# Gated attention followed by graph attention on one core: all five engines in a hand-written order, five x buffers

## The chip, the cores and the metric

The kernel runs on one core of one Trainium2 chip. The metric is the device time of that core in microseconds (us) for one launch over the whole batch.

## The reference

The inputs are `x` (64 graphs of 256 nodes with 512 channels, f32) and an adjacency matrix `adj` (64 x 256 x 256, int32). Cut to what matters:

```python
h = relu(layernorm(x))                                  # layer 0
q, k, v = h @ Wq.T, h @ Wk.T, h @ Wv.T                   # 8 heads of 64 channels
c = softmax(where(adj, q @ k.T / 8, -inf)) @ v
gate = sigmoid(concat(c, h) @ Wg.T + bg)
x = x + gate * h + (1 - gate) * c
h = relu(layernorm(x))                                  # layer 1
Wh = h @ W
e = leaky_relu((Wh @ a1)[:, None] + (Wh @ a2)[None, :])
x = x + elu(softmax(where(adj, e, -1e9)) @ Wh)
```

## The kernel before, in words

All work is in f32. A graph's 256 nodes fill two tiles of 128 partitions. The five dense products (q with k, v, gate, Wh) are done by a Strassen-like scheme, `strassen`: seven products (`product`, line 149) instead of eight, in three PSUM banks `ma`, `mb`, `mc`. Each of these banks has one buffer. The scheme is cut into three parts: products 1, 6, 5, then 7, 2, then 4, 3. VectorE (`add`, line 159) and ScalarE (lines 163 and 173) read partial results out of the banks, and the next product into the same bank, or into that bank for the next dense product, has to wait for them. The other PSUM tiles share a pool `w` with five buffers. The sums of operand blocks are made by GpSimd for activations (`token_sums`, lines 133 to 136) and by VectorE for weights (`weight_sums`, lines 104 to 107, once at the start).

The batch is a software pipeline. Round `i` works on four graphs: `p = i + 1` (transposes of h, q, k, v), `i` (attention), `q = i - 1` (gate, residual, second norm, Wh) and `r = i - 2` (graph attention, output). In round `i` the kernel loads graph `i + 2` into an x buffer, and `p_norm` makes its mask, its statistics and h. The graph is stored from the same buffer at the end of `g_out` four rounds later, when it is graph `r`. The x pool has four buffers and the adj pool one. So the load of graph `i + 2` writes the buffer from which graph `i - 2` is stored in the same round.

The order of TensorE's instructions is the written order of `emit_round`. The order on VectorE (DVE), ScalarE (ACT), GpSimd (POOL) and SyncE (SP) is set by a planner with costs and priorities:

```python
    with tc.manual_schedule(engines={mybir.EngineType.PE}):
```

Names that the prediction uses, with the lines of the kernel before: `norm_stats` (188 to 195), h (203), copies out of PSUM (122 on ScalarE, 124 on VectorE), scores `ps` (276), softmax over scores (294 the masked minimum on VectorE, 298 the exponential on ScalarE, 302 the reciprocal on VectorE, 306 the scaling on GpSimd), transposed probabilities `ptr` and `ptr_l` (315), weighted sum `pc` (336), the difference `d` of `g_mix` (365), the edge terms of `g_edges` (396 to 409), the output products `po` (420) and the ELU with the store (425 to 432).

At the start all twelve weight transfers, the two rows of `a` and the bias are issued on ScalarE's queue (lines 97, 115, 118), and all weight sums and edge columns (line 486) are traced ahead of the first round.

Of the kernel before, what the change touches and what calls it, by code (L numbers as in the profile page):

```python
# [8 lines left out]
F32 = mybir.dt.float32  # L9
I32 = mybir.dt.int32  # L10
BF16 = mybir.dt.bfloat16
AF = mybir.ActivationFunctionType
ALU = mybir.AluOpType
# [9 lines left out]
def kernel(  # L23
# [41 lines left out]
    def pool(name, bufs, **kw):  # L65
# [2 lines left out]
    const = pool("const", 1)  # L68
    st = pool("st", 4)
    sb = {tag: pool(tag, bufs) for tag, bufs in {  # L70
        "x": 4, "adj": 1, "mask": 4, "hT": 3, "S": 3, "qk": 3, "v": 2, "wh": 1, "e": 4, "eT": 4,
        "cT": 1, "z": 1, "tmp": 9, "U": 3,
    }.items()}
    ps = {tag: pool(f"ps_{tag}", bufs, space=bass.MemoryType.PSUM) for tag, bufs in {
        "ma": 1, "mb": 1, "mc": 1, "w": 5,
# [13 lines left out]
        nc.sync.dma_start(at, adj[g].rearrange("(t p) n -> p t n", p=P))  # L89
        graphs[g] = {"x": xt, "adj": at}  # L90

    load_graph(0)

    def load_weight(name, src, extra):
        w = const.tile([P, HC, 2, HH + extra], F32, name=name)
        for n in range(2):
            nc.scalar.dma_start(w[:, :, n, :HH], src[:, n * HH:(n + 1) * HH].rearrange("(c p) f -> p c f", p=P))
        return w

    def weight_sums(name, w):  # L100

        t = const.tile([P, 3, 2, w.shape[3]], F32, name=f"{name}_t")
        b11, b12, b21, b22 = (w[:, r:r + 2, n, :] for r in (0, 2) for n in range(2))
        nc.vector.tensor_tensor(t[:, 1], b22, b12, ALU.subtract)
        nc.vector.tensor_tensor(b12, b12, b11, ALU.subtract)
        nc.vector.tensor_tensor(t[:, 0], b22, b12, ALU.subtract)
        nc.vector.tensor_tensor(t[:, 2], b21, t[:, 0], ALU.subtract)
        return {1: b11, 2: b21, 3: b22, 4: t[:, 2], 5: b12, 6: t[:, 0], 7: t[:, 1]}

    sources = {"q": wqT, "k": wkT, "v": wvT, "gc": wgT[:H], "gh": wgT[H:], "1": w1}  # L110
    loaded = {key: load_weight(f"w{key}_sb", src, key == "1") for key, src in sources.items()}
    weight = {}
    a_sb = [sb["tmp"].tile([P, H], F32, tag="t", name=f"a_sb_{side}") for side in range(2)]
    for side in range(2):
        nc.scalar.dma_start(a_sb[side], bass.AP(tensor=a.tensor, offset=a.offset + side * H, ap=[[0, P], [1, H]]))
    hbg = const.tile([P, HC], F32, name="hbg")
    with nc.allow_non_contiguous_dma(reason="512 biases, once"):
        nc.scalar.dma_start(hbg, bg.rearrange("(c p) -> p c", p=P))

    def evac(dst, src, on_act):  # L120
        if on_act:
# [61 lines left out]
    def norm_stats(xt, name):  # L183

        mv = st.tile([P, NT, 2], F32, tag="mv", name=f"mv_{name}")
        for t in range(NT):
            bs = st.tile([P, 6], F32, tag="bs", name=f"bs_{name}_{t}")
            nc.vector.bn_stats(bs, xt[:, t, :])  # L188
            nc.vector.bn_aggr(mv[:, t, :], bs)
        ve = st.tile([P, NT], F32, tag="ve", name=f"ve_{name}")  # L190
        nc.vector.tensor_scalar_add(ve, mv[:, :, 1], EPS)  # L191
        rs = st.tile([P, NT], F32, tag="rs", name=f"rs_{name}")
        nc.gpsimd.tensor_tensor(rs, ve, mhalf, ALU.pow)  # L193
        nb = st.tile([P, NT], F32, tag="nb", name=f"nb_{name}")
        nc.vector.scalar_tensor_tensor(nb, mv[:, :, 0], -1.0, rs, ALU.mult, ALU.mult)  # L195
        return rs, nb

    def norm_relu(xt, name):
        rs, nb = norm_stats(xt, name)
        hs = []  # L200
        for t in range(NT):
            h = sb["tmp"].tile([P, H], F32, tag="t", name=f"h_{name}_{t}")
            nc.scalar.activation(h, xt[:, t, :], AF.Relu, bias=nb[:, t:t + 1], scale=rs[:, t:t + 1])  # L203
            hs.append(h)
        return hs
# [11 lines left out]
        return hT  # L217


    def p_norm(g):  # L220
        s = graphs[g]
        mask = sb["mask"].tile([P, NT, N], BF16, tag="t", name=f"mask_{g}")
        nc.vector.tensor_scalar(mask, s["adj"], 0.0, MASKED, ALU.is_equal, ALU.mult)
        s["mask"] = mask
        s["h"] = norm_relu(s["x"], f"l0_{g}")

    def p_transpose(g):
        s = graphs[g]
# [50 lines left out]
                    )  # L279
        s["ps"] = psc  # L280

    def a_softmax(g, half):
        s = graphs[g]
        psc, mask = s.pop("ps"), s["mask"]
        es = s["e", half] = {}
        for jj in range(2):
            low, sums, rec = (
                st.tile([P, 2, NT], F32, tag=tag, name=f"{tag}_{g}_{half}_{jj}") for tag in ("low", "sums", "rec")
            )
            for i in range(2):  # L290
                e = sb["e"].tile([P, NT, N], F32, tag="t", name=f"e_{g}_{half}_{jj}_{i}")
                es[jj, i] = e
                for t in range(NT):
                    nc.vector.tensor_tensor_reduce(  # L294
                        e[:, t, :], psc[jj, i][:, t, :], mask[:, t, :], -SCALE, HUGE, ALU.add, ALU.min,
                        accum_out=low[:, i, t:t + 1],
                    )
                    nc.scalar.activation(  # L298
                        e[:, t, :], e[:, t, :], AF.Exp, bias=low[:, i, t:t + 1], scale=-1.0,
                        accum_out=sums[:, i, t:t + 1],  # L300
                    )
            nc.vector.reciprocal(rec, sums)  # L302
            for i in range(2):
                for t in range(NT):
                    e = es[jj, i]
                    nc.gpsimd.tensor_scalar(  # L306
                        e[:, t, :], e[:, t, :], rec[:, i, t:t + 1], 1.0, ALU.mult, ALU.mult
                    )

    def transpose_probs(e, pool, name, on_act):  # L310

# [37 lines left out]
    def g_gate(g):  # L349
# [5 lines left out]
            f"z_{g}", [P, 2, P], on_channels([(weight["gh"], s["hS"]), (weight["gc"], s["cS"])]), dst  # L355
        )

    def g_mix(g):

        s = graphs[g]  # L360
        hT, cT, z = s["hT"], s["cT"], s["z"]
        for half in (1, 0):
            js = slice(2 * half, 2 * half + 2)
            d = sb["tmp"].tile([P, 2, N], F32, tag="t", name=f"d_{g}_{half}")
            nc.gpsimd.tensor_tensor(d, hT[:, js, :], cT[:, js, :], ALU.subtract)
            for j in (2 * half, 2 * half + 1):
                nc.scalar.activation(z[:, j, :], z[:, j, :], AF.Tanh, bias=hbg[:, j:j + 1], scale=0.5)  # L367
            nc.vector.scalar_tensor_tensor(d, z[:, js, :], 1.0, d, ALU.add, ALU.mult)
            nc.vector.scalar_tensor_tensor(z[:, js, :], d, 0.5, cT[:, js, :], ALU.mult, ALU.add)

    def g_residual(g):
        s = graphs[g]
        for t in range(NT):
            py = ps["w"].tile([P, H], F32, tag="t", name=f"py_{g}_{t}")
            for j in range(HC):
                nc.tensor.transpose(py[:, j * P:(j + 1) * P], s["z"][:, j, t * P:(t + 1) * P], ident)
            nc.vector.tensor_tensor(s["x"][:, t, :], s["x"][:, t, :], py, ALU.add)
        s["h1"] = norm_relu(s["x"], f"l1_{g}")

    def g_transpose_h(g):  # L380
        s = graphs[g]
# [53 lines left out]
    def emit_round(i):  # L435
# [8 lines left out]
        def part(fn, g, n):  # L444
            if 0 <= g < B:
                if n == 0:
                    parts[fn] = fn(g)
                parts[fn][n]()

        p, q, r = i + 1, i - 1, i - 2  # L450
        part(g_gate, q, 0)
        step(g_edges, r)
        part(g_gate, q, 1)
        step(p_transpose, p)
# [1 line left out]
        step(g_mix, q)  # L456
        step(g_transpose, r)
        step(a_transpose, i, 0)
        part(p_qk, p, 0)
        step(g_residual, q)  # L460
        step(g_out, r, 0)
        part(p_qk, p, 1)
        step(a_scores, i, 1)
        step(a_softmax, i, 1)
        step(g_out, r, 1)
        part(p_qk, p, 2)
        step(g_transpose_h, q)
        part(p_v, p, 0)
        step(a_weigh, i, 0)
        part(p_v, p, 1)  # L470
        step(a_transpose, i, 1)
        part(p_v, p, 2)
        step(g_sums, i)
        step(p_norm, p + 1)
        part(g_wh, q, 0)
        step(a_weigh, i, 1)
        part(g_wh, q, 1)
        step(a_scores, p, 0)
        part(g_wh, q, 2)
        step(a_softmax, p, 0)  # L480

    p_norm(0)
    for c in range(HC):
        for side in range(2):
            scr = sb["tmp"].tile([P, 2, HH], F32, tag="t", name=f"scr_{c}_{side}")
            nc.vector.scalar_tensor_tensor(
                scr, loaded["1"][:, c, :, :HH], 1.0, a_sb[side].rearrange("p (n f) -> p n f", n=2),
                ALU.mult, ALU.mult, accum_out=loaded["1"][:, c, side, HH:],
            )
    for key, w in loaded.items():  # L490
        weight[key] = weight_sums(f"w{key}_sb", w)
    nc.vector.tensor_scalar_mul(hbg, hbg, 0.5)

    with tc.manual_schedule(engines={mybir.EngineType.PE}):
        for i in range(-1, B + 2):
            if 0 <= i + 2 < B:
                load_graph(i + 2)
            emit_round(i)
            graphs.pop(i - 2, None)

# [31 lines left out]
```

## Time and profile before

| What | us |
|---|---|
| median of 3 runs | 3758.28 (3757.03 to 3759.89) |
| the profiled execution's own time | 3759.92 |
| its span | 3758.1 |
| TensorE busy (matmul) | 3614.4 |
| VectorE busy | 1968.9 |
| ScalarE busy | 1641.7 |
| GpSimd busy | 1626.0 |

The span runs from the first to the last instruction in the trace; about 1.8 us lie around it. All busy times are of the one core. A matmul's end in the trace is modelled, so two groups of matmuls that overlap in the table of time are running back to back. TensorE does nearly all of its work in f32, and each f32 matmul shows as two instructions; transposes show as one.

### The profile page before, as it was taken

Reading aid. Unit: us, or ns where it says so; the run is one execution under the profiler, and the core shown is the slowest. Engines: PE = TensorE matmul, PEld = TensorE weight load, DVE = VectorE, ACT = ScalarE, POOL = GpSimd, SP = SyncE. Lnnn points to the kernel's source line nnn. Section 1 sums busy time; section 2 is a strip of 40 time slices with the busy share of each in tenths; the row PEclk is TensorE's granted clock in tenths of the full one; section 3 lists DMA queues with packets and bytes.
Section 4 is the critical chain, followed back from the end, with each engine's and each line's share of the span. In section 5 each row is a group of like instructions: output and inputs, shape, how many; then the busy total and the mean of one; then the engine's idle time right before and its main releaser. Section 6 shows DMA issues by size and latency. Waiting matters only on the chain.

```text
span 3758.1 us, 68100 instructions
## 1 busy us (share of the span) xinstructions
PE 3614.4 (96%) x26496; PEld 3118.1 (83%) x26496; DVE 1968.9 (52%) x5609; ACT 1641.7 (44%) x4353; POOL 1626.0 (43%) x2439
## 2 busy tenths in 40 slices
PE   5999999999999999999999999999999999999997
PEld 5888888888888888888888888888888888888885
DVE  4555555555555455555555555555555545555554
ACT  2444444444444444444444444444444444444443
POOL 2444444444444443544444444435444444444443
PEclk9999999999999999999999999999999999999998
DMA  3000000000000000000000000000000000000000
GB/s 110 4 29 26 18 29 26 18 26 24 24 26 18 29 26 18 26 29 18 26 19 29 26 18 29 26 18 26 28 19 26 18 29 26 18 26 29 15 18 17
DMA packets 59697, 95.06 MB, mean 25 GB/s; under 512 B 3824, under 2 KB 26352, under 8 KB 59376
## 3 DMA queue, kind: packets, MB, share of 16 engines
q1 hardware_dynamic: 52224, 83.90, 6.8%
q10 hardware_dynamic: 7152, 6.82, 0.6%
q8 instruction: 209, 3.42, 0.4%
q14 instruction: 112, 0.92, 0.1%
HBM read 57.15 MB, written 33.55 MB: 24 GB/s over the span
## 4 chain that ended last, share of the span: by engine, by line
PE 36%; issue 21%; POOL 15%; DMA 11%; DVE 9%; ACT 8%; POOLq 0%; ACTq 0%; DVEq 0%
PE pmb_z L149 6%; PE pma_z L149 6%; DMA x<-in_x_dram 6%; PE pmb_wh L149 6%; POOL e L306 5%; DMA out_dram<-x 5%; ACT e L298 4%; PE ps L276 3%; PE pc L336 3%; PE pmc_z L149 3%; PE pmc_wh L149 3%; ACT h_l L203 2%; POOL rs_l L193 2%; POOL x L430 2%; DVE bs_l L188 2%
## 5 line engine op out<-in xcount | busy, mean ns | idle before, releaser
L306 POOL TENSOR_SCALAR e<-e,rec 128x256 f32<-128x256 f32 x1024 | 497.2, 504 | 314.9 <-DVE rec L302 299.6
L298 ACT ACTIVATE e<-e,low 128x256 f32<-128x256 f32 x1024 | 505.5, 495 | 115.5 <-DVE low L294 115.5
L193 POOL TENSOR_TENSOR rs_l<-ve_l,mhalf 128x2 f32<-128x2 f32 x128 | 90.4, 706 | 956.3 <-DVE ve_l L191 956.3
L203 ACT ACTIVATE h_l<-x,nb_l,rs_l 128x512 f32<-128x512 f32 x256 | 194.5, 807 | 635.4 <-DVE nb_l L195 630.3
L294 DVE CUSTOM_DVE_ANT_0 e<-ps,mask 128x256 f32<-128x256 f32 x1024 | 369.0, 416 | 69.7 <-PE ps L276 67.0
L430 POOL TENSOR_TENSOR x<-x,pos 128x512 f32<-128x512 f32 x128 | 162.7, 1271 | 246.4 <-DVE pos L429 246.4
L122 ACT COPY eT<-ptr 128x512 f32<-128x512 f32 x512 | 261.5, 593 | 11.1 <-PE ptr L315 3.7
L276 PE MATMUL ps<-qk 64*128 64x256 f32 x2048 | 255.7, 389 | 0.0
L315 PE MATMUL ptr<-ident,e 128*128 128x128 f32 x2048 | 247.9, 274 | 3.9 <-POOL e L306 2.7
L420 PE MATMUL po<-wh,eT_l 128*128 128x512 f32 x512 | 249.1, 609 | 2.0 <-DVE low L294 1.2
L336 PE MATMUL pc<-eT,v 128*64 128x256 f32 x2048 | 249.3, 385 | 0.0
L188 DVE BATCH_NORM_STATS2 bs_l<-x 128x6 f32<-128x512 f32 x256 | 168.5, 679 | 140.0 <-DMA x<-in_x_dram 140.0
L315 PEld LDWEIGHTS ptr<-ident,e 128*128 128x128 f32 x2048 | 230.2, 141 | 13.3 <-POOL e L306 6.4
L122 ACT COPY cT<-pc 128x512 f32<-128x512 f32 x128 | 74.9, 585 | 372.8 <-PE pc L336 372.8
L405 ACT ACTIVATE eg<-eg,nm 128x256 f32<-128x256 f32 x128 | 64.0, 501 | 381.3 <-DVE nm L402 381.3
L276 PEld LDWEIGHTS ps<-qk 64*128 64x128 f32 x2048 | 187.3, 186 | 46.8 <-issue 22.1
L336 PEld LDWEIGHTS pc<-eT,v 128*64 128x64 f32 x2048 | 135.6, 136 | 98.2 <-issue 42.7
L149 PE MATMUL pmb_wh<-w_sb_t,S_l 128*128 128x257 f32 x512 | 145.2, 406 | 64.9 <-DVE v L159 60.0
L159 DVE TENSOR_TENSOR u_wh<-pmb_wh,u_wh 128x257 f32<-128x257 f32 x128 | 54.6, 427 | 288.6 <-PE pmb_wh L149 217.8
L135 POOL TENSOR_TENSOR S_l<-hT_l 128x256 f32<-128x256 f32 x128 | 93.7, 732 | 253.1 <-DVE hT_l L124 253.1
L159 DVE TENSOR_TENSOR u_v<-pmb_v,u_v 128x256 f32<-128x256 f32 x128 | 54.4, 425 | 279.8 <-PE pmb_v L149 211.4
L367 ACT ACTIVATE z<-z,hbg 128x256 f32<-128x256 f32 x256 | 116.3, 501 | 183.6 <-DVE z L159 183.6
(143 smaller groups left out, 8710.7 us busy)
## 6 DMA issues: line engine op xcount, KB each, us to landing
x<-in_x_dram SPq DMA_DIRECT2D x64, 512.0 KB, 3.6
out_dram<-x SPq DMA_DIRECT2D x64, 512.0 KB, 2.8
adj<-in_adj_dram SPq DMA_DIRECT2D x64, 256.0 KB, 2.7
wq_sb<-in_L_gnn_Wq_dram ACTq DMA_DIRECT2D x2, 512.0 KB, 7.5
wk_sb<-in_L_gnn_Wk_dram ACTq DMA_DIRECT2D x2, 512.0 KB, 12.1
wv_sb<-in_L_gnn_Wv_dram ACTq DMA_DIRECT2D x2, 512.0 KB, 12.2
wgc_sb<-in_L_gnn_Wg_dram ACTq DMA_DIRECT2D x2, 512.0 KB, 8.7
wgh_sb<-in_L_gnn_Wg_dram ACTq DMA_DIRECT2D x2, 512.0 KB, 8.9
```

What stands on the lines that cost most here:

```text
L122: nc.scalar.copy(dst, src)
L149: nc.tensor.matmul(bank[key][(slice(None), *cols)], lhsT, rhs, start=first and i == 0, stop=last and i == len(todo) - 1, skip_group_check= ...
L188: nc.vector.bn_stats(bs, xt[:, t, :])
L203: nc.scalar.activation(h, xt[:, t, :], AF.Relu, bias=nb[:, t:t + 1], scale=rs[:, t:t + 1])
L276: nc.tensor.matmul(psc[jj, i][:, t, :], qk[r:r + DK, 0, jj, t * P:(t + 1) * P], qk[r:r + DK, 1, jj, :], start=True, stop=True,)
L294: nc.vector.tensor_tensor_reduce(e[:, t, :], psc[jj, i][:, t, :], mask[:, t, :], -SCALE, HUGE, ALU.add, ALU.min, accum_out=low[:, i, t:t + 1],
L298: nc.scalar.activation(e[:, t, :], e[:, t, :], AF.Exp, bias=low[:, i, t:t + 1], scale=-1.0, accum_out=sums[:, i, t:t + 1],)
L306: nc.gpsimd.tensor_scalar(e[:, t, :], e[:, t, :], rec[:, i, t:t + 1], 1.0, ALU.mult, ALU.mult)
L315: nc.tensor.transpose(pt[:, kc, t * P:(t + 1) * P], e[:, t, kc * P:(kc + 1) * P], ident)
L336: nc.tensor.matmul(pc[i * DK:(i + 1) * DK, jj, :], s["v"][:, kc, hd * DK:(hd + 1) * DK], eT[jj, i][:, kc, :], start=(kc == 0), stop=(kc == ...
L420: nc.tensor.matmul(pm, s["egT"][:, kc, t * P:(t + 1) * P], s["wh"][:, kc, :, :HH], start=(kc == 0), stop=(kc == NT - 1))
L430: nc.gpsimd.tensor_tensor(s["x"][:, t, :], s["x"][:, t, :], pos, ALU.add)
```

## The change

Every engine, and the queue of SyncE, now follows the written order, and the written order is made finer:

- x has five buffers instead of four, the pool `tmp` eight instead of nine.
- `load_graph(i + 2)` becomes the first step of round `i`.
- The softmax of half a set of heads is two steps with two heads each. The second step of the first half runs in the next round, behind part 1 of the gate. The steps of the second half stand on both sides of the second output step.
- `p_norm` is split: mask and statistics (`p_stats`) come before `a_transpose(i, 1)`, h (`p_norm`) behind part 1 of Wh. `g_residual` loses h to a step `g_norm` behind the first output step. `g_mix` loses the difference `d` to a step `g_diff` before `g_edges`, and takes the halves in the order 0, 1.
- The transfers of Wq and Wv go to SyncE's queue, Wk stays on ScalarE's, and the gate's weights, W, `a` and the bias go to SyncE's queue at round 0. The weight sums are placed just ahead of their first use in rounds -1 and 0, the edge columns in round 0.
- `weight_sums` computes the same values from other operands (`t[0] = t[1] + b11`), with the same four instructions.

The diff, cut to its core:

```diff
-        "x": 4, "adj": 1, "mask": 4, "hT": 3, "S": 3, "qk": 3, "v": 2, "wh": 1, "e": 4, "eT": 4,
-        "cT": 1, "z": 1, "tmp": 9, "U": 3,
+        "x": 5, "adj": 1, "mask": 4, "hT": 3, "S": 3, "qk": 3, "v": 2, "wh": 1, "e": 4, "eT": 4,
+        "cT": 1, "z": 1, "tmp": 8, "U": 3,
...
         nc.vector.tensor_tensor(t[:, 1], b22, b12, ALU.subtract)
+        nc.vector.tensor_tensor(t[:, 0], t[:, 1], b11, ALU.add)
         nc.vector.tensor_tensor(b12, b12, b11, ALU.subtract)
-        nc.vector.tensor_tensor(t[:, 0], b22, b12, ALU.subtract)
         nc.vector.tensor_tensor(t[:, 2], b21, t[:, 0], ALU.subtract)
...
+    def p_stats(g):
+        s = graphs[g]
+        s["mask"] = sb["mask"].tile([P, NT, N], BF16, tag="t", name=f"mask_{g}")
+        nc.vector.tensor_scalar(s["mask"], s["adj"], 0.0, MASKED, ALU.is_equal, ALU.mult)
+        s["stats"] = norm_stats(s["x"], f"l0_{g}")
...
         p, q, r = i + 1, i - 1, i - 2
+        step(load_graph, p + 1)
         part(g_gate, q, 0)
+        step(a_softmax, i, 0, 1)
+        step(g_diff, q)
         step(g_edges, r)
         part(g_gate, q, 1)
         step(p_transpose, p)
...
         step(a_transpose, i, 0)
+        if i == -1:
+            weight_sums("q")
+            weight_sums("k")
         part(p_qk, p, 0)
         step(g_residual, q)
         step(g_out, r, 0)
+        step(g_norm, q)
         part(p_qk, p, 1)
         step(a_scores, i, 1)
-        step(a_softmax, i, 1)
+        step(a_softmax, i, 1, 0)
         step(g_out, r, 1)
+        step(a_softmax, i, 1, 1)
         part(p_qk, p, 2)
         step(g_transpose_h, q)
+        if i == -1:
+            weight_sums("v")
         part(p_v, p, 0)
         step(a_weigh, i, 0)
+        if i == 0:
+            weight_sums("gh")
+            weight_sums("gc")
+            nc.vector.tensor_scalar_mul(hbg, hbg, 0.5)
         part(p_v, p, 1)
+        step(p_stats, p + 1)
         step(a_transpose, i, 1)
         part(p_v, p, 2)
+        if i == 0:
+            edge_columns()
+            weight_sums("1")
+        part(g_wh, q, 0)
+        step(p_norm, p + 1)
         step(g_sums, i)
-        step(p_norm, p + 1)
-        part(g_wh, q, 0)
         step(a_weigh, i, 1)
         part(g_wh, q, 1)
         step(a_scores, p, 0)
+        step(a_softmax, p, 0, 0)
         part(g_wh, q, 2)
-        step(a_softmax, p, 0)
...
-    with tc.manual_schedule(engines={mybir.EngineType.PE}):
+    with tc.manual_schedule(engines=None):
+        load_graph(0)
+        load_weight("q", nc.sync)
+        load_weight("k", nc.scalar)
+        load_weight("v", nc.sync)
+        p_stats(0)
+        p_norm(0)
         for i in range(-1, B + 2):
-            if 0 <= i + 2 < B:
-                load_graph(i + 2)
+            if i == 0:
+                load_weight("gh", nc.sync)
+                load_weight("gc", nc.sync)
+                load_weight("1", nc.sync)
+                load_small()
             emit_round(i)
```

TensorE's own steps stand in the same order before and after.

## The prediction

> **What bounds the kernel now.** I read the page's first two parts, then the waits, then two stretches of the timeline.
>
> ```profile
> PE 3614.4 (96%) x26496; PEld 3118.1 (83%) x26496; DVE 1968.9 (52%) x5609; ACT 1641.7 (44%) x4353; POOL 1626.0 (43%) x2439
> PE   5999999999999999999999999999999999999997
> ```
>
> TensorE bounds it. Of 143.7 us without matmul, the stretches show 27.4 + 9.7 before 39.4 us, 78.4 between 165 and 3640 us (60 rounds), the rest mainly at the end. TensorE's work and order don't change, so only these idle times can. The waits name them (total, times, longest):
>
> ```profile
> DVE bs_l L188 <- DMA x<-in_x_dram: 140.0, 61, 5.5
> PE pmb_wh L149 <- DVE v L159: 60.0, 60, 1.0
> PE pt_l L215 <- ACT h_l L203: 28.9, 4, 27.4
> ACT L203 <- DMA wgh_sb<-in_L_gnn_Wg_dram: 25.2, 1, 25.2
> PE pmc_v L149 <- DVE v L159: 17.1, 37, 1.8
> PE pma_qk L149 <- DVE hT_l L124: 9.5, 1, 9.5
> ```
>
> At the start ScalarE sits behind its own weight transfers until 25.2 us, so h, and TensorE, start late. In each round VectorE waits for x. One round's timeline shows what follows:
>
> ```profile
> 1857.39 0.38 SPq L432 DMA_DIRECT2D out_dram<-x  x1
> 1860.19 0.37 SPq L88 DMA_DIRECT2D x<-in_x_dram  x1
> ...
> 1863.68 0.69 DVE L188 BATCH_NORM_STATS2 bs_l<-x 128x6 f32<-128x512 f32 x1 [1.88 <-DMA x<-in_x_dram]
> ...
> 1867.19 0.41 DVE L159 TENSOR_TENSOR v<-pmb_v,u_v 128x256 f32<-128x256 f32 x1
> ...
> 1867.74 1.11 PE L149 MATMUL pmb_wh<-w_sb_t,S_l 128*128 128x257 f32 x4 [1.00 <-DVE v L159]
> ```
>
> Graph r is stored, its buffer is reloaded, VectorE waits for the load, the sums that empty bank mb come late, and TensorE waits.
>
> **What the Trainium skill says.** "TensorE: Matmul & The Clock Gate", section "Architectural detail", says that ScalarE and VectorE are strict FIFO and that TensorE reorders only weight loads. The trace agrees: sums whose products had long ended stand behind the statistics above. The same page, "Part 1: The HAM clock gate", says that a long idle TensorE runs at half clock for a while; after the idle start eight matmuls take 1.66 us (39.36 to 41.02) instead of 0.89. "SBUF — State Buffer", section "SBUF: two separate sides", says that a DVE instruction with two SBUF inputs and a GpSimd one lock each other out; here line 400 took 0.69 us normally and at most 0.83, beside a GpSimd `d`. "DMA: Bandwidth & Descriptors", section "Queues, rings and completion order", says that queues take turns on the same engines; at the start both together moved 322 GB/s.
>
> **The change, part by part.**
>
> *Five x buffers, earlier loads.* The load of i + 2 now needs the store of i - 3, made in the round before, so store and reload (some 6 us) leave the path. `p_stats` finds its data. The clean round from 1833.62 to 1890.81 took 57.19 us. In it Wh's products 1 to 6 start 2.02 apart instead of 0.87 (1.15 lost) and v's products 4 to 3 0.97 instead of 0.86 (0.11). Without both a round is 57.19 - 1.15 - 0.11 = 55.93. The chain's repeated mark gives a mean round of 57.55, so 1.62 us a round are at stake, 97 in 60 rounds. SP passes nothing that waits: adj's one buffer was read in the round before.
>
> *New wait at the gate.* VectorE now does, in this order: gate's first sum; four masked minima, a reciprocal that waits for ScalarE; the edge terms, a second reciprocal that waits for ScalarE; only then the sum of product 7, which product 4 in bank mb needs. Before, that sum stood ahead of the second reciprocal, and the softmax was over:
>
> ```profile
> 1881.05 0.42 DVE L159 TENSOR_TENSOR u_z<-pmb_z,u_z 128x256 f32<-128x256 f32 x1 [1.71 <-PE pmb_z L149]
> ...
> 1883.00 0.87 DVE L399 SCALAR_TENSOR_TENSOR eg<-pe,wh,mask 128x256 f32<-128x256 f32 x2 [1.53 <-PE pe L396]
> ...
> 1885.45 0.41 DVE L159 TENSOR_TENSOR u_z<-pmb_z,u_z 128x256 f32<-128x256 f32 x1
> ...
> 1886.76 0.17 DVE L409 RECIPROCAL rec<-sums 128x2 f32<-128x2 f32 x1 [0.43 <-ACT eg L405]
> ...
> 1887.25 1.06 PE L149 MATMUL pmb_z<-hT_l,wgh_sb_t 128*128 128x128 f32 x8
> ```
>
> Start to start, from the same trace: 1881.05 + 0.34 to the minima + 2.56 to their reciprocal (0.46 to the first exponential, three more at 0.49, 0.62 to the reciprocal; 1849.00 to 1851.55 shows the same) + 0.10 to the edges + 0.91 + 0.70 to the maximum + 0.75 to its exponential + 1.13 to the second reciprocal + 0.09 to the sum + 0.55 until TensorE goes on = 1888.18. TensorE would be there at 1887.25: 0.93 lost. `d` and the scaling now run on GpSimd beside line 400: 0.14 more by its longest duration. I take 1.07; the bounds are 0.8 and, with the lock held for a whole `d` (1.27), 2.2.
>
> *New wait at v.* The scores of the second half start at S = 1847.45. VectorE does four minima from S + 1.16 (1848.61), reciprocal 2.56 later, the ELU minimum at 1851.42 when `po` ends (+0.10 or that, whichever is later), sum 1.44 later behind two ScalarE steps, four minima 0.61 later, reciprocal 2.56 later, and only then the sum that frees bank mb for v's product 6: 1856.13, TensorE goes on 0.80 later, 1856.93, against 1856.51. 0.42 lost; 0.2 to 0.8. Before it, the residual's chain (two x sums, statistics, ELU, h's factor, two sums of q and k) ends at 1848.3, 0.3 before the scores need VectorE.
>
> So a round loses 1.49 instead of 1.62: 0.13 x 60 = 8 us gained (from -60 to +37 at the ends).
>
> *Other moved steps.* These cost nothing, and the cover is named. Product 7 of q/k and of Wh, and product 4 of q/k: their sums end 1 to 4 us before. Gate's product 6 needs Wh's last sums, which end 1.2 us before. GpSimd: `d` (2 x 1.27) ends before the sums of hT can start; the sums for Wh are done 5 us before Wh, since S_g no longer mixes with them. ScalarE's copies out of bank ma have over 1 us. `tmp` with eight buffers: twelve tiles a round, and the tile eight places earlier is always dead by then.
>
> *Start.* x lands at 5.5, adj at 7.6 us as before (two queues share as before). Mask and statistics: 0.43 + 2 x 0.78 + 0.2 to 9.9, power on GpSimd (1.07) and factor to 11.2; ScalarE is free, having issued only Wk. h until 12.8, transposes in the slow clock and copies (3.4 us from h's start to the copy's, 0.6 for the copy) until 15.3. Estimate for Wk, at half of 322 GB/s: 10.5 us, as Wq landed before; Wq on SP behind x and adj: 0.5 MB by then, the rest at the full rate, 12.5. Products of q and k start at 15.3 instead of 39.36: 24 us. Given back: Wv's two sums ahead of product 6 of v (1.4); the statistics of graph 1, h and the split softmax ahead of the first transposed probabilities (1.3); in round 0 edge columns 8 x 0.61 and sums of W 4.0 stand ahead of the softmax and thus of gate's first sum: VectorE gets there at 107.6 on before's axis, TensorE wants product 7 at 104.43 and gets it at 108.15 (3.7), and restarts slowly (1.5). The sums of the gate's weights (5.1) fit between v's products. 24 - 7.9 = 16 us gained; bounds 8 and 22.
>
> *End.* Round 63 loses less to GpSimd's mixed sums (2), round 64 more to the late sum (1): 1 gained.
>
> **Sum.** 3759.92 (the profiled execution; the median lies 1.6 lower) - 8 - 16 - 1 = 3734.9, as a median 3733. The difference is 0.7%; a measurement here can tell about 0.2% (7.5 us) from no change.
>
> **Rivals.**
> 1. *VectorE's order holds nothing back* (the waits at gate and v don't appear, because an exponential comes sooner or TensorE is late itself). Then all 97 go: 3759.92 - 97 - 17 - 1.6 = 3644. For: VectorE is 52% busy. Against: the durations above. Near it lies that the order isn't kept on all engines and only the fifth buffer acts. Together 0.09.
> 2. *Start limited by DMA.* If Wq lands at 20 us, the start brings 8 less, and a gate wait longer by 0.2 takes 62 x 0.2 = 12: 3733 + 20 = 3753. For: DMA is at full load until 27 us. Against: Wq and Wk go first now. 0.14.
> 3. *Slower: the lock at line 400.* If it waits for a whole `d`, the gate loses 1.13 more, 62 rounds: 3733 + 70 = 3803. It decides from 0.4 us more a round (25/62). For: the order puts `d` and scaling right beside it. Against: beside scaling, line 429 took 0.72 instead of 0.69. 0.13.
> The forecast itself: 0.64, its own range 3714 to 3750.
>
> **Numbers.** Faster: 0.64 + 0.09 + 0.04 of rival 2 = 0.77. Same: 0.10. Slower: 0.13. The range leaves 0.1 on each side: 3706 to 3762.
>
> **What would show it.** Right: no VectorE wait for x after the start; no `pmb_wh` wait; instead TensorE `pmb_z` waits for VectorE `u_z` about 60 times with some 0.9, and `pmb_v` for `qk` with some 0.3 visible; first matmul near 12 us, `pma_qk` near 15, a wait of `pmb_z` of 3 to 4 us in round 1. Wrong: a round other than 55.9 plus those waits; a wait over 1.5 us at the gate; line 400 over 1 us.

## The result, and the profile after

The forecast was 3733 us, faster. The changed kernel takes **3790.64 us** (median of 4 runs, 3789.13 to 3791.08) against 3757.66 (3755.55 to 3759.89) for the kernel before on the same chip: a ratio of 1.0087, interval 1.007 to 1.0104. It is slower by 33 us, and outside the range. The profiled execution took 3790.4 us, its span is 3788.6.

The first two parts of the page after (busy time of each engine; TensorE's busy tenths in 40 slices), and the head of its chain of work that ended last, by engine and by line:

```profile
PE 3622.9 (96%) x26496; PEld 3127.3 (83%) x26496; DVE 1958.6 (52%) x5609; ACT 1650.8 (44%) x4353; POOL 1634.3 (43%) x2439
PE   7999999999999999999999999999999999999997
...
PE 59%; DVE 19%; ACT 19%; issue 2%; POOL 0%; DMA 0%; DVEq 0%; POOLq 0%; ACTq 0%; SPq 0%
```

The same chain of the kernel before:

```profile
PE 36%; issue 21%; POOL 15%; DMA 11%; DVE 9%; ACT 8%; POOLq 0%; ACTq 0%; DVEq 0%
```

The first slice is fuller than before (7 instead of 5): the start did gain. In the chain, DMA (11%) and GpSimd (15%) are gone: as forecast, no round waits for x any more. In their place stand VectorE and ScalarE with 19% each. Their busy time is within 11 us of before's; they are now links between two matmuls. The waits of TensorE after (total, times, longest) say which:

```profile
PE pmb_v L160 <- DVE qk L170: 65.2, 63, 1.1
PE pmb_z L160 <- DVE u_z L170: 50.3, 63, 1.6
PE pt_l L226 <- ACT h_l L214: 15.5, 8, 11.5
PE pmb_z L160 <- POOL S_c L145: 7.8, 1, 7.8
```

Both waits that the forecast named are there, once a round. The gate's (`pmb_z`) shows 0.8 us each time, near the 0.9 of the forecast. The one at v (`pmb_v`) was to be the smaller, with some 0.3 us visible, and shows 1.0.

**Where the time went.** Take as a mark the first gate product of a round (`pma_z<-hT_l,wgh_sb`). In round 2 it starts at 150.72 before and 141.30 after; in round 63 at 3659.05 and 3686.11. So:

| stretch | before | after | difference | forecast |
|---|---|---|---|---|
| up to the mark of round 2 | 150.72 | 141.30 | -9.4 | -16 |
| 61 rounds, each | 57.51 | 58.11 | +0.60 | -0.13 |
| 61 rounds, together | 3508.33 | 3544.81 | +36.5 | -8 |
| after the mark of round 63 | 99.05 | 102.49 | +3.4 | -1 |

The sum, 30.5, is the difference of the two spans. The rounds decide.

### The profile page after: what moved, and what is told of

Read it like the earlier page. It is cut to its first block, busy times and chain, and to the rows that moved or that the text cites. A ratio compares the mean times of both kernels' runs of the same rounds, so it can differ in the third digit from the quotient of the medians.

```text
span 3788.6 us, 68295 instructions
## 1 busy us (share of the span) xinstructions
PE 3622.9 (96%) x26496; PEld 3127.3 (83%) x26496; DVE 1958.6 (52%) x5609; ACT 1650.8 (44%) x4353; POOL 1634.3 (43%) x2439
## 4 chain that ended last, share of the span: by engine, by line
PE 59%; DVE 19%; ACT 19%; issue 2%; POOL 0%; DMA 0%; DVEq 0%; POOLq 0%; ACTq 0%; SPq 0%
ACT e L311 10%; PE pmb_z L160 7%; PE pc L348 6%; PE ptr L327 6%; PE pmb_wh L160 5%; PE pmb_v L160 5%; PE ps L290 3%; PE pmc_z L160 3%; PE pmb_qk L160 3%; PE pma_qk L160 3%; PE pmc_qk L160 3%; PE pma_z L160 3%; PE pmc_wh L160 3%; PE pma_wh L160 3%; PE pmc_v L160 3%; ACT h_l L214 3%
## 5 line engine op out<-in xcount | busy, mean ns | idle before, releaser
L448 ACT ACTIVATE pos<-po,rec 128x512 f32<-128x512 f32 x128 | 88.0, 687 | 513.5 <-DVE neg L446 513.5
L160 PE MATMUL pmb_v<-wv_t,S_l 128*128 128x256 f32 x512 | 144.6, 405 | 66.5 <-DVE qk L170 65.2
L315 DVE RECIPROCAL rec<-sums 128x4 f32<-128x4 f32 x256 | 45.6, 178 | 301.8 <-ACT e L311 301.8
L311 ACT ACTIVATION_READ_ACCUMULATOR e<-e,low 128x1 f32 x1024 | 191.9, 187 | 0.0
L160 PEld LDWEIGHTS pmb_v<-wv_t,S_l 128*128 128x128 f32 x512 | 86.7, 189 | 123.2 <-DVE qk L170 90.5
```

The costliest lines, as they stand in the source:

```text
L160: nc.tensor.matmul(bank[key][(slice(None), *cols)], lhsT, rhs, start=first and i == 0, stop=last and i == len(todo) - 1, skip_group_check= ...
L311: nc.scalar.activation(e[:, t, :], e[:, t, :], AF.Exp, bias=low[:, i, t:t + 1], scale=-1.0, accum_out=sums[:, i, t:t + 1],)
```

## The experiments

All kernels start from the changed one unless stated. A ratio is always to the kernel before, timed beside the run on the same chip (3756.66 to 3758.90 us). "A round" is always the mean of the same 61 rounds, mark to mark, in one trace. The line numbers 446 to 450 are the ELU (425 to 429 before), 420 to 430 the edge terms (399 to 409), 170 VectorE's sums behind the products (159).

**1. Which wait costs what.** Two kernels each take away one of the two, by moving VectorE's work only.

The last softmax step (two heads of the second half) goes behind the sums that v waits for:

```diff
-        step(a_softmax, i, 1, 1)
         part(p_qk, p, 2)
+        step(a_softmax, i, 1, 1)
```

> The second softmax step of the second half moves behind the last part of q and k; nothing else differs from the changed kernel. Theory: the sums that empty bank mb no longer stand behind a softmax, the pmb_v wait (1.21 a round) goes, the pmb_z wait stays: 3790.6 - 1.21 x 63 = about 3714 us. Rival (the wait comes from late scores or from ScalarE, and moves on with the softmax to a_transpose or to the second sums of v): at most half of it goes, above 3750 us.

Measured 3709.27 us, ratio 0.9867 (0.9852 to 0.9882), a round 56.78. The waits of TensorE:

```profile
PE pmb_z L160 <- DVE u_z L170: 49.8, 63, 1.6
PE pt_l L226 <- ACT h_l L214: 16.3, 8, 11.5
```

`pmb_v`'s wait for `qk` is gone from the list and the gate's wait is untouched. The wait at v therefore cost 58.11 - 56.78 = 1.33 us a round, not 0.42.

At the gate, VectorE stands 1.22 us in front of the second reciprocal, and the sum that TensorE needs stands behind it (the changed kernel):

```profile
1835.73 1.04 PE L226 MATMUL pt_l<-ident,h_l 128*128 128x128 f32 x8
...
1837.00 0.17 DVE L430 RECIPROCAL rec<-sums 128x2 f32<-128x2 f32 x1 [1.22 <-ACT eg L426]
1837.08 0.40 DVE L170 TENSOR_TENSOR u_z<-pmb_z,u_z 128x256 f32<-128x256 f32 x1
...
1837.54 1.16 PE L160 MATMUL pmb_z<-hT_l,wgh_t 128*128 128x128 f32 x8 [0.78 <-DVE u_z L170]
```

Only this reciprocal, which waits for ScalarE's exponentials, moves behind that sum:

```diff
-        rec = st.tile([P, NT], F32, tag="rec1", name=f"rec1_{g}")
-        nc.vector.reciprocal(rec, sums)
-        s["eg"], s["rec1"] = e, rec
+        s["eg"], s["sums1"] = e, sums
+
+    def g_rec(g):
+        s = graphs[g]
+        rec = s["rec1"] = st.tile([P, NT], F32, tag="rec1", name=f"rec1_{g}")
+        nc.vector.reciprocal(rec, s["sums1"])
...
         part(g_gate, q, 1)
+        step(g_rec, r)
```

> Only the reciprocal of the edge sums moves, behind the gate's second part; nothing else differs from the changed kernel. Theory (VectorE stands 1.2 us in front of this reciprocal, waiting for ScalarE, with the gate's sum queued behind it): the sum runs right behind the maximum, the pmb_z wait goes: about 3790.6 - 58 = 3733 us, as with the softmax put back. Rival (the softmax in front of the edges, or the port, is enough to be late): half or less goes, above 3760 us.

("The port" in this expectation is the lock between VectorE and GpSimd that the prediction names.) Measured 3725.58 us, ratio 0.991 (0.9893 to 0.9926), a round 57.08. Of the two waits only v's is left:

```profile
PE pmb_v L160 <- DVE qk L170: 66.5, 63, 1.1
```

An instruction that runs 0.17 us cost 58.11 - 57.08 = 1.03 us a round by where it stood in VectorE's queue.

Both together:

> Both single cures of the written order together: the reciprocal of the edge sums behind the first gate part (e8) and the sums of the q/k products ahead of the second scaled rows (e2). If the two waits are separate stalls of TensorE, their gains add: 3790.6 - 65.0 - 81.4 = 3644 us (3638 to 3652), below the kernel before and some 7 us below before's order with five x buffers. If one wait only hands over to the other or to a third, the time stays above 3690 us.

Measured **3644.0** us (3642.98 to 3645.05), ratio 0.9701 (0.9686 to 0.9715), a round 55.74. The gains add: 1.03 + 1.33 = 2.36, and 58.11 - 55.74 = 2.37. Neither wait handed over to a third; the largest waits of TensorE that are left come 8 times and once:

```profile
PE pt_l L226 <- ACT h_l L214: 15.6, 8, 11.6
PE pmb_z L160 <- POOL S_c L145: 7.9, 1, 7.9
```

**2. Why the wait at v is three times the forecast.** The timeline after, in the middle of the run (start, us, engine, line; in brackets the idle time before and who ended it), around the second ELU of a round:

```profile
1859.32 0.72 DVE L446 TENSOR_SCALAR neg<-po,rec 128x512 f32<-128x512 f32 x1
...
1860.08 0.69 ACT L448 ACTIVATE pos<-po,rec 128x512 f32<-128x512 f32 x1 [0.88 <-DVE neg L446]
...
1860.66 0.62 ACT L449 ACTIVATE neg<-neg 128x512 f32<-128x512 f32 x1
...
1861.32 0.69 DVE L450 SCALAR_TENSOR_TENSOR pos<-neg,pos 128x512 f32<-128x512 f32 x1 [1.27 <-ACT neg L449]
...
1864.49 0.18 DVE L315 RECIPROCAL rec<-sums 128x4 f32<-128x4 f32 x1 [1.11 <-ACT e L311]
1864.58 0.66 DVE L170 TENSOR_TENSOR qk<-pmb_qk,u_qk 128x512 f32<-128x512 f32 x1
...
1865.30 0.91 PE L160 MATMUL pmb_v<-wv_t,S_l 128*128 128x256 f32 x3 [1.05 <-DVE qk L170]
```

VectorE's minimum (446) and ScalarE's relu (448) both only read `po`, yet the relu starts when the minimum has ended. The exponential stands behind the relu on ScalarE, and VectorE, which is in order, waits for the exponential. From the start of the minimum to that of the sum (450) it is 2.00 us. The forecast had 1.44. To test it, the relu reads x instead of `po`, so that it has nothing to wait for (the kernel's output is then another one, its work the same):

```diff
-        nc.scalar.activation(pos, pm, AF.Relu, scale=r)
+        nc.scalar.activation(pos, s["x"][:, t, :], AF.Relu, scale=r)
```

> In the output step ScalarE's Relu reads x in SBUF instead of the product in PSUM, so that it doesn't wait for VectorE's minimum over the same PSUM bank; the output's positive part is therefore another value. Theory (the forecast mis-sized the ELU: 2.00 us from the minimum to the sum instead of 1.44, in both output steps, because the two readers of one bank take turns): Relu runs beside the minimum, the pmb_v wait falls from 1.21 to about 0.42, 3790.6 - 0.8 x 63 = about 3740 us. Rival (the ELU takes 2.00 us because ScalarE is busy or slow): no change, 3785 to 3795 us.

Measured 3733.61 us, ratio 0.9932 (0.9917 to 0.9947), a round 57.22. In the timeline of this kernel the relu now starts ahead of the minimum:

```profile
1832.36 0.71 ACT L448 ACTIVATE pos<-x,rec 128x512 f32<-128x512 f32 x1
...
1832.70 0.75 DVE L446 TENSOR_SCALAR neg<-po,rec 128x512 f32<-128x512 f32 x1
...
1833.48 0.63 ACT L449 ACTIVATE neg<-neg 128x512 f32<-128x512 f32 x1 [0.42 <-DVE neg L446]
...
1834.15 0.71 DVE L450 SCALAR_TENSOR_TENSOR pos<-neg,pos 128x512 f32<-128x512 f32 x1 [0.70 <-ACT neg L449]
```

and among its waits of TensorE:

```profile
PE pmb_z L160 <- DVE u_z L170: 50.0, 63, 1.6
...
PE pmb_v L160 <- DVE qk L170: 11.0, 63, 0.7
```

1832.70 to 1834.15 is 1.45 us: with the two reads apart, the forecast's 1.44 comes true, the wait at v falls from 65.2 to 11.0 us, and a round gets 58.11 - 57.22 = 0.89 shorter. The gap between 1.33 measured and 0.42 forecast is 0.91. This one term accounts for it: what is left of the wait at v costs 57.22 - 56.78 = 0.44 a round.

**3. Is the order of the softmax at the gate the cause of that wait?** The other way to free VectorE there is to put the first half's second softmax step back into the round before:

```diff
-        step(a_softmax, i, 0, 1)
...
         part(g_wh, q, 2)
+        step(a_softmax, p, 0, 1)
```

> The second softmax step of the first half goes back to the end of the round before, behind the last part of Wh; nothing else differs from the changed kernel. Theory (VectorE's written order makes both waits): the edge terms then start when their transposes end, the late sum of the gate is ready before TensorE wants it, the pmb_z wait (0.93 a round) goes, the pmb_v wait (1.21) stays: 3790.6 - 0.93 x 62 = about 3733 us. Rival (GpSimd's d and scaling beside the edge terms make the gate wait[...]): d still runs there, most of the wait stays: above 3770 us.

Measured 3786.43 us, ratio 1.0071 (1.0056 to 1.0086), a round 58.02: a miss. The wait at the gate is still there (44.7 us). This kernel's timeline says why:

```profile
1886.43 2.50 POOL L375 TENSOR_TENSOR d<-hT_l,cT 128x512 f32<-128x512 f32 x2
...
1887.77 1.72 DVE L421 SCALAR_TENSOR_TENSOR eg<-eg 128x512 f32<-128x512 f32 x1
...
1891.42 0.17 DVE L430 RECIPROCAL rec<-sums 128x2 f32<-128x2 f32 x1 [1.22 <-ACT eg L426]
1891.51 0.40 DVE L170 TENSOR_TENSOR u_z<-pmb_z,u_z 128x256 f32<-128x256 f32 x1
```

The edges come as early as meant, but now the leaky relu (421) runs beside GpSimd's differences `d` and takes 1.72 us. In the changed kernel it runs beside the scaling and ends before `d` begins:

```profile
1833.59 2.28 POOL L318 TENSOR_SCALAR e<-e,rec 128x256 f32<-128x256 f32 x4 [4.91 <-DVE rec L315]
...
1834.29 0.77 DVE L421 SCALAR_TENSOR_TENSOR eg<-eg 128x512 f32<-128x512 f32 x1
...
1835.83 2.50 POOL L375 TENSOR_TENSOR d<-hT_l,cT 128x512 f32<-128x512 f32 x2
```

Whether `d` is the cause was tested by moving `d` alone, in the kernel just shown, from the start of the next round to a place ahead of the last scaling:

```diff
-        step(g_diff, q)
...
+        step(g_diff, i)
         step(a_softmax, p, 0, 1)
```

> The order of e1_softmax_back, and in it GpSimd's two differences d (L375, 2 x 1.25 us) moved ahead of the last scaling of the probabilities, so that no GpSimd instruction with two SBUF inputs runs beside the leaky relu. Theory A (in e1 the wait on u_z stayed because the leaky relu took 1.72 us instead of 0.7 beside d): the leaky relu falls to 0.7 us or less, the reciprocal comes 1.0 us sooner, the 0.7 us wait of the second gate part is gone in 63 rounds, and the time is 3786.4 - 45 = 3741 us (3735 to 3748). Theory B (the wait does not depend on d): no change, 3782 to 3790 us.

Measured 3725.79 us, ratio 0.9918 (0.9901 to 0.9934), a round 57.06. The leaky relu in that kernel (shortest, median and longest duration in ns):

```profile
L421 DVE SCALAR_TENSOR_TENSOR eg<-eg x64: 691/691/693, 149.2 to 3706.2; 128x512 f32<-128x512 f32 x64
```

and in the kernel of the run before it:

```profile
L421 DVE SCALAR_TENSOR_TENSOR eg<-eg x64: 692/1709/1816, 147.3 to 3762.3; 128x512 f32<-128x512 f32 x64
```

Only `d` moved, and a median of 1709 ns became 691; no GpSimd instruction runs beside the leaky relu any more. The round is 0.96 us shorter than without that move (58.02), which is the 1.02 us that the leaky relu got shorter, less 0.06. The gain, 60.6 us, is more than the 45 expected: all of the stall went, and not only its visible part. The mechanism of the forecast's third rival exists, then, with 1.02 us a round; the changed kernel just does not meet `d` there, because its softmax step holds the edges back until the scaling runs.

The two softmax moves together, before that was known:

> Both moves of the two single experiments on the softmax: the first half's second step back to the end of the round before, the second half's second step behind the last part of q and k. Theory: neither wait is left, a round takes about 55.95 to 56.1 us, 3790.6 - 58 - 76 = about 3657 us. Rival (each move only shifts a wait, and together they show a third one): above 3690 us.

Measured 3706.88 us, ratio 0.9862 (0.9848 to 0.9877), a round 56.70, not the 55.95 to 56.1 expected: the gain of the move at v and next to nothing (0.08) from the one at the gate, for the reason just shown.

**4. What the fifth buffer does.** Once the changed kernel with four buffers, where the load has to stand behind the store:

```diff
-        "x": 5, "adj": 1, "mask": 4, "hT": 3, "S": 3, "qk": 3, "v": 2, "wh": 1, "e": 4, "eT": 4,
+        "x": 4, "adj": 1, "mask": 4, "hT": 3, "S": 3, "qk": 3, "v": 2, "wh": 1, "e": 4, "eT": 4,
...
-        step(load_graph, p + 1)
...
         step(g_out, r, 1)
+        step(load_graph, p + 1)
```

> The changed kernel with four x buffers again; the load of graph i + 2 is written behind the store of graph i - 2 (ahead of it, SyncE's queue would stand still). Theory: in the written order the statistics come so late in the round that store (about 1864.4) plus 2.8 plus 3.7 gives 1870.9 against 1871.1 where VectorE wants x: at most some tenths a round, 3785 to 3810 us. Rival (the fifth buffer is what the change lives on): VectorE waits for x as before, a wait of 1 us a round on top of the two, 3850 us or more.

Measured 3790.64 us, ratio 1.0084 (1.0068 to 1.0101), a round 58.11, as with five: the store is issued at 1863.89 in one round, the load at 1866.68, and VectorE reaches the mask at 1871.57 without a wait. The margin is small: in 11 other rounds the mask waits for the adjacency matrix, 4.9 us in all, which TensorE doesn't show (the longest of the 12 below, 7.3, is at the start).

```profile
DVE mask L234 <- DMA adj<-in_adj_dram: 12.2, 12, 7.3
```

And the kernel before, its order left to the planner, with five (and the changed kernel's eight `tmp` buffers):

```diff
-        "x": 4, "adj": 1, "mask": 4, "hT": 3, "S": 3, "qk": 3, "v": 2, "wh": 1, "e": 4, "eT": 4,
-        "cT": 1, "z": 1, "tmp": 9, "U": 3,
+        "x": 5, "adj": 1, "mask": 4, "hT": 3, "S": 3, "qk": 3, "v": 2, "wh": 1, "e": 4, "eT": 4,
+        "cT": 1, "z": 1, "tmp": 8, "U": 3,
```

> The kernel before with five x buffers and eight tmp buffers, its planner's order otherwise. Theory: the wait for x is the whole of its 1.62 us a round, so 3757.7 - 97 = about 3661 us, faster than the changed kernel. Rival (the planner puts the statistics or the softmax elsewhere and makes another wait, or x was not the cause): 3720 us or more.

Measured 3651.02 us, ratio 0.9713 (0.9699 to 0.9728), a round 55.74. Of VectorE's 140.0 us of waits for x one of 5.2 us is left, at the start:

```profile
DVE bs_l L188 <- DMA x<-in_x_dram: 5.2, 1, 5.2
```

So in the written order, with its two stalls, the late place of the statistics already does what the fifth buffer is for, and in the planner's order five buffers are enough for 107 us. Two things are not separated here. With five buffers the planner also orders VectorE otherwise (the statistics of x stand right behind the residual's, no longer among the sums of v), so the 107 us belong to the buffer together with that order. And four buffers in the written order without the two stalls were not run: there the mask comes 6.4 us behind the store (1848.88 to 1855.24) instead of 7.7, while in the run with four buffers the load of x was issued 2.8 us behind the store, that of the adjacency matrix 0.5 behind it, and the matrix landed 4.1 later (median). An estimate from these is that VectorE would wait about 1 us a round. The written order without its two stalls and the planner's order with five buffers have the same round, 55.74.

**5. The start.** In round 0 VectorE computes edge columns and W's sums ahead of the factor that h of graph 2 needs. After:

```profile
85.58 1.52 ACT L214 ACTIVATE h_l<-x,nb_l,rs_l 128x512 f32<-128x512 f32 x2 [11.50 <-DVE nb_l L210]
...
87.01 0.56 ACT L133 COPY cT<-pc 128x512 f32<-128x512 f32 x1
...
89.23 2.08 PE L160 MATMUL pmb_z<-S_c,wgc_t 128*128 128x128 f32 x8 [7.82 <-POOL S_c L145]
```

ScalarE stands 11.5 us in front of h; the copy of cT, GpSimd's sums of it and the gate's product 6 stand behind h. The run below puts h of graph 2 ahead of the edge columns in round 0:

> The changed kernel with h of graph 2 written ahead of the edge columns and the sums of W in round 0. Theory (in round 0 ScalarE stands in front of h, whose factor VectorE makes behind 9 us of weight work, and cT, its sums and the gate's product 6 stand behind it: 7.8 us at pmb_z and a slow restart): the 7.8 us go, but VectorE is still late for the first masked minima, so product 7 waits about 4 to 5 us instead: 3790.6 - 5 = about 3786 us. Rival (S_c is late because of GpSimd's own slow sums): no change in the place of the wait.

Measured 3788.72 us, ratio 1.008 (1.0065 to 1.0095), 1.9 us less instead of the 5 expected, which lies within what a measurement can tell; the mark of round 2 comes at 139.35 instead of 141.30. That wait is nearly gone (1.0), and a wait of 5.7 us for `u_z` behind the same columns takes most of its place; 4 to 5 were expected. On top of the moves of both experiment 1 kernels, with h now right behind the statistics:

> As the run with both cures, and in round 0 the normalization of graph 2 ahead of the edge columns and the first GAT weight sums. The start's wait for the token sum falls from 7.8 to about 1 us as it did alone (3790.6 to 3788.7): 3642 us, 2 us below the run with both cures; if the restart of TensorE is what costs and not the wait, no difference.

Measured **3640.45** us (3639.31 to 3642.0), ratio 0.9692 (0.9677 to 0.9706), against 3644.0: a difference of 3.6 us, 0.1%, where 2 were expected. The mark of round 2 comes 1.6 us sooner (139.40 against 140.99), and the rounds are the same. This version beats both kernels, the one before by 3.1%.

## Why the prediction was wrong, step by step

- **What bounds it, and the load of x: right.** No VectorE wait for x and no `pmb_wh` wait are left. The clean round was given as 55.93 and is 55.74 (two kernels). What the step did not see is that the changed kernel does not need the fifth buffer for it (experiment 4).
- **New wait at the gate, 1.07: right.** The chain was to bring TensorE on at 1888.18 instead of 1887.25, 0.93 late. In the trace the transposes ahead of it start at 1835.73 and are issued in 0.88, so product 4 could start at 1836.61; it starts at 1837.54, 0.93 late. The next group follows after 1.00 instead of 0.89, which makes 1.04; without the wait a round is 1.03 shorter. The mechanism is the forecast's, the closeness of the sum partly luck: the 0.14 for line 400 was 0.08 (0.77 against 0.69), TensorE went on 0.46 behind the sum, not 0.55, and the slower second group was not in it.
- **New wait at v, 0.42: this term failed.** It is 1.33. The step had the sum follow the ELU minimum by 1.44 us, that is, ScalarE's relu beside VectorE's minimum; it is 2.00, because the relu waits for the minimum. The term counts twice. At the second ELU of the round it stands directly in the chain: 0.56. At the first ELU (2.02, from 1852.41 to 1854.43) it stands ahead of the softmax of the scores, which start at 1855.02: the first minima follow 1.41 after them (1856.43; forecast 1.16), 0.25 more. With h and copies late on ScalarE their reciprocal comes 2.79 later (1859.22; forecast 2.56), 0.23 more. Of these 1.04 the forecast had already spent 0.15 waiting for the end of `po`, and 0.08 were gained at the last sum. That leaves 0.81, and 0.42 + 0.81 is 1.23; in the trace TensorE is 1.21 late in that round (1865.30 instead of 1864.09). The next group follows after 0.97 instead of 0.87, which makes 1.31; the mean over the rounds is 1.33. The trace before spoke against the 1.44: in none of its 128 pairs did the relu begin before the minimum had ended, and from minimum to sum it was never less than 2.08. In the rounds ScalarE came to the relu late for other reasons, so the wait itself shows only at the end of the run, where nothing else hid it:

```profile
3748.07 0.75 DVE L425 TENSOR_SCALAR neg<-po,rec 128x512 f32<-128x512 f32 x1 [3.76 <-PE po L420]
3748.91 0.69 ACT L427 ACTIVATE pos<-po,rec 128x512 f32<-128x512 f32 x1 [6.29 <-DVE neg L425]
```

- **The other moved steps at no cost: right.** With the two stalls cured, no wait of TensorE that comes back every round is left (experiment 1).
- **The rounds together.** Forecast 57.55 - 1.62 + 1.07 + 0.42 = 57.42; measured 55.74 + 1.03 + 1.33 = 58.10. The error at v (+0.91) outweighs those of the clean round (-0.19) and of the gate (-0.04).
- **The start, 16: too much.** The products of q and k do start 25.5 us sooner (39.36 to 13.88; forecast 24). But 16.1 are given back instead of 7.9. Product 7 of q/k waits 1.66 for Wk's sums: beside GpSimd's token sums four of the eight sums of Wq and Wk take 1.09 to 1.22 us, the other four 0.68. The edge columns and W's sums were costed, but for the gate's product 7 behind them (3.7 + 1.5); the first victim is h, and through it product 6, with 7.8 us and a slow restart: three groups of eight matmuls take 5.28 us (89.23 to 94.51) instead of 3 x 0.89, so 2.6 more. The forecast's example of a slow restart was misread, too: before, the eight matmuls from 39.36 on take 1.87 (until 41.23), not 1.66; at 41.02 the weight loads of the next eight begin. "TensorE: Matmul & The Clock Gate" in the Trainium skill, "Part 1: The HAM clock gate", says that an idle TensorE comes back at half clock; the trace agrees with 1.87 us for the first eight and a granted clock of 0.50 from 89.2 to 94.5. With Wv's 1.33 and a v wait of 0.72 this makes 14.1. Of the other 2.0, waits for h of graph 1 make 0.8 (0.43 + 0.38), and matmuls that ran slower elsewhere about 1.2 on balance: TensorE's busy time in this stretch is 112.7 instead of 108.9, of which 2.6 are counted above, and around 45 us the granted clock was 0.50 for 6.8 us (43.45 to 50.28), before for 3.4 (68.21 to 71.62).
- **The end, 1 gained: 3.4 lost.** Most of it goes with the same pair of stalls in the last rounds: without them the end takes 100.2 instead of 102.5.
- **The rivals.** The first, that VectorE's order holds nothing back, was put at 3644: that is what the run with both moves measures (3644.0). The agreement to the microsecond is luck: its round is shorter (55.74 against 55.93) and its start gains less than the rival's sum had, and it is another kernel; in the changed kernel VectorE's order does hold TensorE back. The second, a start limited by DMA, was not it; VectorE limited the start. The third, slower by the lock at line 400, named the right side and the wrong place. In the range of the rounds, -60 takes 2.2 at the gate with 0.42 at v; with 0.8 at v it would be -83.

## What to carry to other kernels

An instruction's price in a hand-written order is not its duration but how long its engine stands in front of it: put what waits for another engine (a reciprocal of sums that ScalarE is still making) behind the sums that free a bank for TensorE. Before costing a chain across engines, look whether two steps that seem to run side by side read the same tile, and find a place in the trace where nothing else hides it. And ask of each buffer added whether the new order still needs it: here the order with the late statistics did without.

## What the runs showed of the hardware

- Two engines that only read one PSUM tile took turns: ScalarE's relu of `po` waited for VectorE's minimum of it 127 times in the changed kernel and began 0.04 us (median) after the minimum's end. Whether the hardware or only the program's semaphores ask for it is not shown; that it costs 0.55 us a chain is (2.00 against 1.45).
- The leaky relu, a VectorE instruction whose two inputs are both in SBUF, takes 0.69 us alone and 1.71 (median of 62 rounds) when it meets GpSimd's differences, which have two SBUF inputs. "SBUF — State Buffer" in the Trainium skill, section "SBUF: two separate sides", describes an exclusive lock held for a whole instruction against any GpSimd instruction that reads SBUF. The 1.72 shown agrees: it starts 0.09 us after the second difference must have (1886.43 + 1.25), and ends 0.56 after that one's end at 1888.93, about as if it had only run then. In the changed kernel GpSimd is the one that waits: the leaky relu takes 0.77 beside the scaling (one SBUF tile), and the one scaling that begins while it runs takes 0.91 instead of 0.48, in all of 62 rounds.
